# A four-layer graph network on one core: a pair's score vector reaches all partitions through DRAM instead of TensorE transposes

## The chip, the core and the metric

The kernel runs on one core of a Trainium2 chip. The time is that of the device for one launch, in microseconds, and the median of three launches is given. The core has five engines with an instruction queue each: TensorE (PE: matrix products and transposes, which write to PSUM), VectorE (DVE), ScalarE (ACT), GpSimd (POOL) and SyncE (SP), whose queue issues almost all DMA transfers of this kernel. Each of SBUF's and PSUM's 128 partitions holds one row of a tile. [...]

## The reference

`x` is 128 graphs of 128 nodes with 512 features, and `adj` is a 128x128 matrix for each graph. Four layers follow one another, and each ends with a residual sum and a layer norm. Two of them build a score for each pair of nodes out of two vectors, one value per row and one per column:

```python
# layer 0
Xw = X @ Wv + bv
sj = Xw @ aw[:d, 0]
si = Xw @ aw[d:, 0]
e = leaky_relu(sj[:, None, :] + si[:, :, None] + ab[0], negative_slope=0.2)
alpha_matrix = A * exp(e)
transition = alpha_matrix / (sum(alpha_matrix, axis=-1, keepdims=True) + 1e-12)
for k in range(3):
    H = H + Xk @ Wk[k] + bk[k]
    Xk = einsum('bij,bjd->bid', transition, Xk)
# x = layernorm(x + relu(H))

# layer 2
y = x @ w
s = y @ a
A = s[..., :, None] + s[..., None, :]
A = tanh(A / 8.0) * 8.0
A = where(A >= 0, A, 0.1 * A)
A = exp(A) * A_shape
A = A / sum(A, axis=-1, keepdims=True)
A = A * sum(A_shape, axis=-1, keepdims=True)
out = A @ x @ w
```

Layer 1 is a hypergraph convolution and layer 3 is attention with eight heads. The change doesn't touch them. In the kernel, layers 2 and 3 run as one stage.

## The kernel before

The kernel handles graphs in pairs (`U = 2`), so each layer has 64 pairs, and two pairs at a time go through its stages together. It is written as a list of operations with keys, which a planner in the kernel puts into one order for each engine before the program is built. The planner also gives the operations their buffers. A tile of the kind `four` is 128 partitions of 1024 floats, `sq` holds a pair's two 128x128 matrices, `col` holds a few numbers per partition, and `bank` is one buffer of PSUM.

```python
U = 2
BUFS = 12
SQS = 8          # buffers of kind sq
COLS = 32
ROWS = 4         # buffers of kind row (512 floats)
...
WHEN0 = (-3.0, -1.6, -1.0, 0, 0)              # keys of the stages of layer 0
WHENT = (.8, 2.1), (2.0, 3.1)                 # layer 0: scores of the two pairs; their use
WHEN2 = (-2.4, -2.0, -1.45, -1.15, -.7, .3, .5, 2)   # stages of layers 2 and 3
```

A key counts in pairs. The first number of `WHEN2` is for the loads of layer 2, the second for its scores, the third for the first product with the finished matrix.

This brings a pair's score vector to all partitions. A column of 128 values, one in each partition, is read as a 128x128 matrix whose columns are all alike; its transpose has that vector in every row:

```python
def spread_pair(srcs):
    pt = bank()
    with plan.together():
        for b, s in enumerate(srcs):
            pe.transpose(pt[:, b * P:(b + 1) * P], s, ident)
    return pt
```

Layer 0 uses it as follows. `R[r]` is the result of the product with the weights, and two of its columns are the scores `sj` (column `3 * P`) and `si` (column `3 * P + 1`):

```python
twice(left, WT["0"], QW, ...)           # two-level Strassen product, seven parts, .28 apart
yield
for r, i in enumerate(both):
    A = load_adj(i)
    plan.key = base + WHENT[0][r]
    s = col(U)
    ac.activation(s, R[r][:, :, 0, 3 * P + 1], AF.Identity, bias=c0)
    pt = spread_pair([R[r][:, b, 0, 3 * P:3 * P + 1].to_broadcast([P, P]) for b in range(U)])
    e = sq()
    for b in range(U):
        ac.activation(e[:, b], pt[:, b * P:(b + 1) * P], AF.Prelu, bias=s[:, b:b + 1], alpha=0.2)
    ac.activation(e, e, AF.Exp)
    den = col(U)
    ...                                  # times A, row sums, reciprocal, scaling (DVE, POOL)
    loads.append(through_dram(e.rearrange("p b (k w) -> p b k w", w=Q), f"e{i}"))
for r, i in enumerate(both):
    plan.key = base + WHENT[1][r]
    x0 = load_rows(x[i:i + U].rearrange("b p f -> p b f"))
    TT = pair_turned(loads[r])           # back from DRAM, transposed by DVE
    for m in (1, 0):
        for b in range(U):
            ...
            pe.matmul(by, TT[:, b], of, start=False, stop=True, skip_group_check=True)
```

Layer 2 uses it as follows:

```python
s2 = col(U)
for b in range(U):
    dot(s2[:, b:b + 1], x2[:, b], wa_b)              # DVE, sum into one value per row
deg = col(U)
ve.tensor_reduce(deg, A, AX.X, OP.add)
pt = spread_pair([s2[:, b:b + 1].to_broadcast([P, P]) for b in range(U)])
F = sq()
for b in range(U):
    ac.activation(F[:, b], pt[:, b * P:(b + 1) * P], AF.Tanh, bias=s2[:, b:b + 1])
ac.activation(F, F, AF.Prelu, alpha=0.1)
ac.activation(F, F, AF.Exp, scale=8.0)
...                                                  # times A, row sums, scaling (DVE, POOL)
FTs.append(through_dram(F.rearrange("p b (k w) -> p b k w", w=Q), f"F{i}", False))
...
FT = pair_turned(load)                               # the next stage
pe.matmul(pt[:, c * P:(c + 1) * P], x2[:, b, c * P:(c + 1) * P], FT[:, b], start=True, stop=True)
```

`through_dram` writes a matrix to DRAM in blocks and gives a function that loads it back with the blocks rearranged; `pair_turned` then transposes 32x32 blocks on DVE. All instructions are called from one line of the planner, so the profile gives them all the line L369, and they are told apart by their tiles.

Of the kernel before, what the change touches and what calls it, by code (L numbers as in the profile page):

```python
# [13 lines left out]
AF = mybir.ActivationFunctionType  # L14
# [3 lines left out]
P = 128  # L18
# [7 lines left out]
EPS = 1e-5  # L26
U = 2
BUFS = 12
SQS = 8
COLS = 32  # L30
ROWS = 4
KS = 4
OUTS = 4

# [3 lines left out]
WHEN1 = (-3.0, -2.3, -1.6, -1.1, .2, .6)  # L38
STEP1 = .22
WHENH, WHENW, WHENG = (2.4, 3.0), (2.9, 3.6), (3.6, 4.3)  # L40
WHEN2 = (-2.4, -2.0, -1.45, -1.15, -.7, .3, .5, 2)
WHENV, WHENS, WHENP, WHENO = (.9, 1.9), (2.2, 3.2), (3, 4), (3.5, 4.5)
LAG1, LAG2 = 1, 1.5
SOFT = .2
# [333 lines left out]
def kernel(  # L378
# [21 lines left out]
    for kind, (n, _) in spans.items():  # L400
        places[kind] = [first[:, at(kind, k):at(kind, k) + SIZE[kind]] for k in range(n)]
        if kind != "w7":
            for k in range(n):
                later[kind, k] = [(old, i) for old in (("q3", "h") if kind == "q7" else ("w7",))
                                  for i in range(spans[old][0])
                                  if at(old, i) < at(kind, k) + SIZE[kind] and at(kind, k) < at(old, i) + SIZE[old]]
    slots = {"w7": 7, "out": OUTS, "q7": 0, "q3": 0, "h": 0, "w28": 0, "sq": SQS, "col": COLS, "row": ROWS, "bank": 6, "t0": 1, "t1": 1,
             "four": BUFS, "row1": 1, "k": KS}
# [11 lines left out]
    for kind, k, t in (*(("out", k, t) for k, t in enumerate(outs)), ("w28", 0, places["w28"][0]),  # L420
                       ("row1", 0, places["row1"][0])):
        for c in range(SIZE[kind] // SIZE["four"]):
            later["four", len(places["four"])] = [(kind, k)]
            places["four"].append(t[:, c * SIZE["four"]:(c + 1) * SIZE["four"]])
    plan = Plan(slots, later)
    pe, ve, ac, po, sp = (plan.engine(*e) for e in ((PE, nc.tensor), (DVE, nc.vector), (ACT, nc.scalar),
                                                     (POOL, nc.gpsimd), (SP, nc.sync)))

    def tile_of(kind, *shape):
        n = math.prod(shape)  # L430
        flat = View(Tile(kind), np.arange(SIZE[kind]))[:, :n]
        names = [f"a{k}" for k in range(len(shape))]
        return flat if len(shape) == 1 else flat.rearrange(
            f"p ({' '.join(names)}) -> p {' '.join(names)}", **dict(zip(names, shape)))
# [5 lines left out]
    def bank():  # L440
        return tile_of("bank", D)

    def four():

        return tile_of("four", U, D)

    def sq(n=P):
        return tile_of("sq", U, n)

    def col(*n):  # L450
        return tile_of("col", *n)
# [3 lines left out]
    ident = View(Tile("fixed", ident_), np.arange(P))  # L455
# [9 lines left out]
    def row():  # L465
        return tile_of("row", D)
# [205 lines left out]
    def scratch(name, *shape):  # L672
        t = tc.dram_tile(list(shape), FP, name=name)
        return Tile("dram", t)

    def part(tile, how, first, n=1):
        return View(tile, np.arange(first, first + n), (how,))
# [22 lines left out]
    def from_dram(src, kind):  # L700

        nj, _, n = src.shape
        t = kind().rearrange("p u f -> p (u f)").rearrange("p (m j w) -> p m j w", m=4, j=nj)
        for j in range(nj):
            with plan.together():
                for k in range(4):
                    sp.dma_start(t[k * Q:(k + 1) * Q, :, j],
                                 src[j].rearrange("(m r) (k w) -> k r m w", r=Q, k=4)[k],
                                 run=n // 4, parts=Q)
        return t.rearrange("p m j w -> p (m j w)")  # L710
# [64 lines left out]
                for d, v, y in zip(sides(*((0, 1), (1, 1))[j == T3]), sides(1, 0), sides(1, 1)):  # L775
                    po.tensor_tensor(d, v, y, OP.add)

    def spread_pair(srcs):
        pt = bank()
        with plan.together():  # L780
            for b, s in enumerate(srcs):
                pe.transpose(pt[:, b * P:(b + 1) * P], s, ident)
        return pt

    def pair_turned(load):
        t = sq()
# [14 lines left out]
    bias = row().rearrange("p (h n i) -> p h n i", h=2, n=2)  # L801
# [92 lines left out]
    def layer0(i0):  # L894


        both = [i0 + U * r for r in range(2)]
        xbs = [from_dram(x[i:i + U], four) for i in both]
        yield
        xT, loads = [], []  # L900
        for xb in xbs:
            xT.append(four().rearrange("p u (c n) -> p u c n", n=P))
            turned(xT[-1].rearrange("p u c n -> p (u c) n"), xb)
        yield
        left = lefts(xT)
        yield
        base = plan.key
        add = ve.tensor_tensor
        R = [tile_of("out", U, 4, QW) for _ in range(2)]

        def fresh(bs):
            def takes(d):
                def put(d, b):
                    def run(p):
                        ac.copy(d[:, P:], p[:, P:])
                        add(d[:, :P], p[:, :P], b, OP.add)
                    return run
                d11, d12, d21, d22 = d
                return plain_take(*d) | {"p1": put(d11, bs[:, 0]), "v": put(d12, bs[:, 1]),
                                         "p5": put(d22, bs[:, 1]), "c21": put(d21, bs[:, 0])}  # L920
            return takes

        twice(left, WT["0"], QW, lambda r, half: [R[r][:, b, 2 * half + n] for b in range(U) for n in range(2)],
              lambda r, half: [R[r][:, b, 2 * half:2 * half + 2] for b in range(U)],
              [fresh(bias[:, half]) for half in range(2)], .28)
        yield
        loads = []
        for r, i in enumerate(both):
            A = load_adj(i)
            plan.key = base + WHENT[0][r]  # L930
            s = col(U)
            ac.activation(s, R[r][:, :, 0, 3 * P + 1], AF.Identity, bias=c0)
            pt = spread_pair([R[r][:, b, 0, 3 * P:3 * P + 1].to_broadcast([P, P]) for b in range(U)])
            e = sq()
            for b in range(U):
                ac.activation(e[:, b], pt[:, b * P:(b + 1) * P], AF.Prelu, bias=s[:, b:b + 1], alpha=0.2)
            ac.activation(e, e, AF.Exp)
            den = col(U)
            for b in range(U):
                ve.scalar_tensor_tensor(e[:, b], e[:, b], 1.0, A[:, b], op0=OP.mult, op1=OP.mult,  # L940
                                        accum_out=den[:, b:b + 1])
            ac.activation(den, den, AF.Identity, bias=tiny)
            ve.reciprocal(den, den)
            for b in range(U):
                po.tensor_scalar(e[:, b], e[:, b], den[:, b:b + 1], None, op0=OP.mult)
# [4 lines that stand above are left out]
            TT = pair_turned(loads[r])  # L950
            for m in (1, 0):
                for b in range(U):
                    p = tile_of(("t0", "t1")[b], D)
                    by = p.rearrange("p (q i) -> p q i", i=P)
                    to, of = (R[r][:, b, :, k * P:(k + 1) * P] for k in (m, m + 1))
                    ac.copy(by, to)
                    pe.matmul(by, TT[:, b], of, start=False, stop=True, skip_group_check=True)
                    if m:
                        ac.copy(to, by)
                    else:  # L960
                        ve.scalar_tensor_tensor(x0[:, b], p, 0.0, x0[:, b], op0=OP.max, op1=OP.add)
                        layer_norm(x0[:, b])
                plan.key += .2
            sp.dma_start(x1d[i // U], x0)
# [151 lines left out]
    cols = fixed(2, C, name="cols2")  # L1116
# [51 lines left out]
    def layer23(i0):  # L1168
# [10 lines left out]
        for i, x2, A in each(both, x2s, As):  # L1179
            s2 = col(U)  # L1180
            for b in range(U):
                dot(s2[:, b:b + 1], x2[:, b], wa_b)
            deg = col(U)
            ve.tensor_reduce(deg, A, AX.X, OP.add)
            pt = spread_pair([s2[:, b:b + 1].to_broadcast([P, P]) for b in range(U)])
            F = sq()
            for b in range(U):
                ac.activation(F[:, b], pt[:, b * P:(b + 1) * P], AF.Tanh, bias=s2[:, b:b + 1])
            ac.activation(F, F, AF.Prelu, alpha=0.1)
            ac.activation(F, F, AF.Exp, scale=8.0)  # L1190
            r = col(U)
            for b in range(U):
                ve.scalar_tensor_tensor(F[:, b], F[:, b], 1.0, A[:, b], op0=OP.mult, op1=OP.mult,
                                        accum_out=r[:, b:b + 1])
            ve.reciprocal(r, r)
            for b in range(U):
                po.tensor_scalar(F[:, b], F[:, b], r[:, b:b + 1], deg[:, b:b + 1], op0=OP.mult, op1=OP.mult)
            FTs.append(through_dram(F.rearrange("p b (k w) -> p b k w", w=Q), f"F{i}", False))
        yield
        opss = []  # L1200
        for load, x2 in each(FTs, x2s):
            FT = pair_turned(load)
            GT = four().rearrange("p u (c n) -> p u c n", n=P)
            for b in range(U):
                pt = bank()
# [24 lines left out]
        vs = [four() for _ in range(2)]  # L1230
        base = plan.key - WHEN2[6]

# [93 lines left out]
    n = B // U  # L1326
# [21 lines left out]
    for job, start, step in ((prepare2, 2 * n + LAG1 - .3, .1), (prepare_w, 2 * n + LAG1, 0),  # L1348
                             (prepare3, 2 * n + LAG1 + 2, .1)):
        plan.key = start  # L1350
        for k, _ in enumerate(job()):
            plan.key = start + step * (k + 1)
    layer(layer23, 2 * n + LAG1 + LAG2, WHEN2, ramp, size=2)
    ctx.enter_context(tc.manual_schedule())
# [29 lines left out]
```

## Time and profile before

| | us |
|---|---|
| median of three launches | 5482.09 |
| lowest, highest | 5477.86, 5486.19 |
| span of the profiled launch | 5477.4 |
| PE busy in it | 5346.1 |
| DVE busy | 4549.0 |
| POOL busy | 4037.1 |
| ACT busy | 2397.3 |

By the instructions in it, layer 0 takes the span up to about 1400 us, layer 1 up to about 3100 us, and layers 2 and 3 the rest. Between them lie stretches in which weights are prepared. The page gives an engine's busy time as the union of its instructions' times; matrix products overlap in TensorE, so a product's own duration is longer than the time until the next one starts. PEld is the loading of the stationary operand, which overlaps with PE as well. A name such as `bank<-ident,col` is the tile written, then the tiles read, without buffer numbers. The idle time ahead of an instruction is put down to whatever event came last before it began. A DMA's landing is counted from its issue to its completion.

### The profile page before, as it was taken

The numbers are of one execution on the slowest core, as the hardware profiler recorded it, in microseconds if no ns is written. First come the engines' busy times: TensorE is split into PE (matmuls) and PEld (weight loads), VectorE is DVE, ScalarE is ACT, GpSimd is POOL, SyncE is SP. The second block draws the span as 40 slices with busy tenths as digits, with TensorE's granted clock in tenths as the row PEclk, the third lists the DMA queues.
The fourth block names the chain that finished last, engine by engine and source line by source line (L and its number), as shares of the span: only waits on it lengthen the run. The fifth ranks groups of instructions, "written<-read, shape, count | busy, mean of one in ns | idle before, by whom it ended". The sixth has DMA issues, their size and how long they took to land.

```text
span 5477.4 us, 94041 instructions
## 1 busy us (share of the span) xinstructions
PE 5346.1 (98%) x29145; PEld 4258.7 (78%) x29145; DVE 4549.0 (83%) x11553; ACT 2397.3 (44%) x6479; POOL 4037.1 (74%) x4835
## 2 busy tenths in 40 slices
PE   7999999999999999999999999999999999999998
PEld 4555555555788888888888789899999999999987
DVE  6888887878998899998999978777778777877876
ACT  2444343444443434443434345444455445445444
POOL 6666666666777777777777567777777777777776
PEclk8999999999999999999999999999999999999999
DMA  3333333334554544544454545554454555555553
GB/s 92 98 100 98 104 94 107 93 98 126 153 152 144 155 141 151 155 144 151 149 151 148 161 132 164 160 163 153 161 162 155 162 164 152 161 165 156 161 155 119
DMA packets 788381, 768.35 MB, mean 140 GB/s; under 512 B 264859, under 2 KB 592547, under 8 KB 787878
## 3 DMA queue, kind: packets, MB, share of 16 engines
q1 hardware_dynamic: 786374, 759.71, 45.3%
q8 instruction: 231, 3.78, 0.3%
q10 hardware_dynamic: 1504, 2.62, 0.2%
q14 instruction: 272, 2.23, 0.1%
HBM read 435.83 MB, written 326.24 MB: 139 GB/s over the span
## 4 chain that ended last, share of the span: by engine, by line
PE 56%; DVE 7%; DMA 3%; POOL 2%; issue 1%; ACT 1%; SPq 1%; DVEq 0%; POOLq 0%; ACTq 0%
PE bank L369 42%; PE t L369 14%; DVE first L369 2%; DVE col L369 2%; DVE out L369 1%; DVE four L369 1%; POOL out L369 1%; SPq L369 1%; DMA out<-h 1%; DMA h<-first 1%; DMA out<-x3d 1%; POOL first L369 0%; DMA first<-x3d 0%; ACT first L369 0%; DVE junk L369 0%
## 5 line engine op out<-in xcount | busy, mean ns | idle before, releaser
L369 PE MATMUL bank<-first,four 128*128 128x386 f32 (+3 forms) x5176 | 1438.1, 431 | 32.5 <-DVE out L369 14.2
L369 PEld LDWEIGHTS bank<-first,four 128*128 128x128 f32 (+2 forms) x5176 | 846.3, 187 | 588.6 <-DVE out L369 141.5
L369 DVE TENSOR_TENSOR out<-bank,out 128x386 f32<-128x386 f32 (+1 forms) x1884 | 926.6, 509 | 275.5 <-PE bank L369 215.6
L369 POOL TENSOR_TENSOR out<-out 128x256 f32<-128x256 f32 (+3 forms) x482 | 548.6, 1149 | 297.3 <-DVE out L369 214.0
L369 POOL TENSOR_TENSOR col<-col,neghalf 128x1 f32<-128x1 f32 x640 | 378.8, 597 | 375.6 <-DVE col L369 373.9
L369 DVE TENSOR_TENSOR first<-bank,first 128x256 f32<-128x256 f32 x1362 | 542.1, 412 | 129.6 <-PE bank L369 99.0
L369 PE MATMUL bank<-first,out 128*128 128x256 f32 (+2 forms) x2560 | 623.4, 381 | 25.7 <-DVE first L369 10.1
L369 PEld LDWEIGHTS bank<-first,out 128*128 128x128 f32 (+1 forms) x2560 | 469.4, 190 | 127.3 <-DVE first L369 30.6
L369 PE MATMUL bank<-four,out 128*128 128x256 f32 (+2 forms) x2118 | 538.1, 376 | 2.9 <-DVE col L369 1.4
L369 DVE TENSOR_TENSOR four<-bank,four 128x256 f32<-128x256 f32 x818 | 337.7, 417 | 142.9 <-PE bank L369 128.3
L369 PE MATMUL bank<-out,first 128*128 128x128 f32 (+2 forms) x2840 | 427.8, 290 | 2.2 <-DVE out L369 1.2
L369 ACT COPY out<-bank 128x258 f32<-128x258 f32 (+2 forms) x555 | 236.6, 431 | 419.7 <-PE bank L369 378.6
L369 PEld LDWEIGHTS bank<-four,out 128*128 128x128 f32 (+2 forms) x2118 | 369.7, 189 | 59.1 <-issue 8.4
L369 PEld LDWEIGHTS bank<-out,first 128*128 128x128 f32 (+1 forms) x2840 | 374.4, 188 | 26.0 <-DVE four L369 2.8
L369 ACT ACTIVATE col<-col,col 128x1 f32<-128x1 f32 x640 | 183.2, 292 | 456.2 <-POOL col L369 390.1
L369 POOL TENSOR_TENSOR four<-four,four 128x256 f32<-128x256 f32 (+2 forms) x395 | 329.0, 837 | 13.0 <-DVE four L369 3.2
L369 ACT COPY t<-out 128x512 f32<-128x512 f32 x256 | 150.2, 591 | 421.9 <-DVE four L369 217.6
L369 POOL TENSOR_TENSOR first<-first 128x512 f32<-128x512 f32 (+3 forms) x196 | 232.2, 1197 | 110.3 <-DVE first L369 73.9
L369 POOL TENSOR_TENSOR out<-out,out 128x256 f32<-128x256 f32 (+2 forms) x286 | 288.2, 1011 | 9.3 <-DVE four L369 4.4
L369 POOL TENSOR_TENSOR four<-four 128x256 f32<-128x256 f32 (+2 forms) x331 | 244.3, 754 | 67.6 <-DVE four L369 38.3
L369 POOL TENSOR_SCALAR sq<-sq,col 128x128 f32<-128x128 f32 x256 | 160.5, 636 | 153.4 <-DVE col L369 149.0
L369 DVE BATCH_NORM_STATS2 col<-first 128x6 f32<-128x512 f32 x370 | 245.5, 681 | 27.2 <-ACT first L369 25.4
(406 smaller groups left out, 12715.2 us busy)
## 6 DMA issues: line engine op xcount, KB each, us to landing
h<-first SPq DMA_DIRECT2D x496, 128.0 KB, 2.4
out<-x1d SPq DMA_DIRECT2D x88, 512.0 KB, 4.3
out<-h SPq DMA_DIRECT2D x87, 512.0 KB, 4.6
four<-in_x_dram SPq DMA_DIRECT2D x512, 64.0 KB, 2.0
four<-in_x_dram SPq DMA_DIRECT2D x62, 512.0 KB, 3.5
x1d<-four SPq DMA_DIRECT2D x62, 512.0 KB, 2.7
first<-S SPq DMA_DIRECT2D x61, 512.0 KB, 4.4
out<-S SPq DMA_DIRECT2D x50, 512.0 KB, 4.4
```

The lines of the kernel that those rows point to most:

```text
L369: call(*map(real, args), **{n: real(a) for n, a in kw.items()})
```

## The change

The score vector of a pair is written from its column to a small array in DRAM, one row of 128 values per graph. Then one load reads both rows, 256 values, into every one of the 128 partitions. The tile `sq` that holds them takes the place of the PSUM bank as the source of ScalarE's first operation. This takes the transposes of layers 0 and 2 away from TensorE. The other transposes of the kernel stay, those of weights, of vectors that are spread once, and of the last attention. Two more `sq` buffers are given, two `row` buffers are taken away, and the first two stages of layer 2 are keyed earlier.

```diff
-SQS = 8
+SQS = 10
 COLS = 32
-ROWS = 4
+ROWS = 2
...
-WHEN2 = (-2.4, -2.0, -1.45, -1.15, -.7, .3, .5, 2)
+WHEN2 = (-2.5, -2.2, -1.45, -1.15, -.7, .3, .5, 2)
...
-    def spread_pair(srcs):
-        pt = bank()
-        with plan.together():
-            for b, s in enumerate(srcs):
-                pe.transpose(pt[:, b * P:(b + 1) * P], s, ident)
-        return pt
+    def spread_pair(cols, name):
+
+        d = scratch(name, U, P)
+        sp.dma_start(part(d, lambda t: t.rearrange("b p -> p b"), 0), cols, run=1)
+        t = sq()
+        sp.dma_start(t.rearrange("p b n -> p (b n)"),
+                     part(d, lambda t: t.rearrange("(x b) p -> x (b p)", x=1).to_broadcast([P, U * P]), 0), run=U * P)
+        return t
...
-            pt = spread_pair([R[r][:, b, 0, 3 * P:3 * P + 1].to_broadcast([P, P]) for b in range(U)])
+            pt = spread_pair(R[r][:, :, 0, 3 * P], f"s{i}")
             e = sq()
             for b in range(U):
-                ac.activation(e[:, b], pt[:, b * P:(b + 1) * P], AF.Prelu, bias=s[:, b:b + 1], alpha=0.2)
+                ac.activation(e[:, b], pt[:, b], AF.Prelu, bias=s[:, b:b + 1], alpha=0.2)
...
-            pt = spread_pair([s2[:, b:b + 1].to_broadcast([P, P]) for b in range(U)])
+            pt = spread_pair(s2, f"s2{i}")
             F = sq()
             for b in range(U):
-                ac.activation(F[:, b], pt[:, b * P:(b + 1) * P], AF.Tanh, bias=s2[:, b:b + 1])
+                ac.activation(F[:, b], pt[:, b], AF.Tanh, bias=s2[:, b:b + 1])
```

## The prediction

> **What bounds the kernel now.** I read the page's busy shares first, then the busy time by stage, then every instruction that has `ident` as an operand (the transposes), then stretches of the timeline around single pairs, and last the DMA issues and the waits of the DMA queue. The page:
>
> ```profile
> PE 5346.1 (98%) x29145; PEld 4258.7 (78%) x29145; DVE 4549.0 (83%) x11553; ACT 2397.3 (44%) x6479; POOL 4037.1 (74%) x4835
> ```
>
> The share alone hides stages, so here is the busy time in one stretch each of layer 0, of layer 1 and of layers 2 and 3 (stretch and its length, then PE, PEld, DVE, ACT and POOL busy with their counts, granted clock, DMA share, GB/s):
>
> ```profile
> 500.00:1000.00 500.00, 499.23 (x1489) 270.52 (x1488) 408.08 (x1041) 204.24 (x475) 338.07 (x401) 1.00 0.34 102
> 1600.00:2600.00 1000.00, 981.04 (x4689) 825.43 (x4688) 902.30 (x2231) 405.09 (x760) 775.81 (x909) 1.00 0.50 150
> 3500.00:5000.00 1500.00, 1495.58 (x11102) 1367.17 (x11101) 1196.56 (x3175) 739.98 (x2520) 1161.76 (x1432) 1.00 0.51 160
> ```
>
> In both stages that the change touches TensorE is busy over 99.7% of the time, at full clock. Work taken off it there should leave the span, unless it is replaced by a wait. The other engines have room: DVE is at 82% and 80%, ACT at 41% and 49%, the DMA engines at 34% and 51%.
>
> The transposes, with min/median/max duration, and those who waited for them:
>
> ```profile
> L369 PE MATMUL bank<-ident,out x168: 271/273/473, 55.9 to 5448.1; 128*128 128x128 f32 x168
> ...
> L369 PE MATMUL bank<-ident,col x66: 272/273/323, 3088.4 to 5327.3; 128*128 128x128 f32 x66
> ...
> L369 PE MATMUL t<-ident,col x62: 272/273/273, 3230.9 to 5187.9; 128*128 128x128 f32 x62
> ...
> who waited for it (us, times):
>   ACT sq L369: 137.2, 77
> ```
>
> The 66 + 62 = 128 with `col` are layer 2's (64 pairs of two). Layer 0's are most of the 168 with `out`; the rest of those belong to weights and to the last attention. The 137 us of ACT's waiting cost nothing by themselves: ACT is far from the bound.
>
> The 273 ns of a record is a latency, not what it costs TensorE. That is the distance between starts. A pair in layer 0, and one in layer 2 (start us, us, what):
>
> ```profile
> 738.89 1.14 PE L369 MATMUL bank<-first,four 128*128 128x386 f32 x3
> 739.86 0.38 PE L369 MATMUL bank<-ident,out 128*128 128x128 f32 x2
> 740.08 1.21 PE L369 MATMUL bank<-first,four 128*128 128x386 f32 x3
> ```
>
> ```profile
> 4012.69 0.61 PE L369 MATMUL bank<-out,first 128*128 128x128 f32 x4
> 4013.14 0.38 PE L369 MATMUL bank<-ident,col 128*128 128x128 f32 x2
> 4013.45 0.82 PE L369 MATMUL bank<-out,four 64*128 64x128 f32 x9
> ```
>
> In layer 0 a pair takes 740.08 - 739.86 = 0.22 us of TensorE. In layer 2 it looks like 0.31 us, but what follows are 64-row products of the attention. In eight places of this trace a 64-row group follows an ordinary 128x128 product with no transpose between, and its start is 0.20 us later in place of the usual 0.11. So 0.09 of the 0.31 is the switch to 64 rows, which stays; the pair itself is 0.22 us here too.
>
> **What the Trainium skill says.** (1) "TensorE: Matmul & The Clock Gate", Part 4: PE-mode transpose, gives about 275 ns for a transpose in a kernel's context, mostly access latency. The trace agrees (273 ns), and shows besides that the next instruction starts after 0.11 us, so I don't multiply by 275. (2) "DMA: Bandwidth & Descriptors", Rules for kernel authors: a DMA that reads what an earlier one wrote must wait for that one's completion. So the added path is two whole DMAs in series. (3) The same page, Anatomy of one DMA, puts a fixed cost of about 2 us on each, most of it completion at the target memory. The landings below agree for small transfers (1.5 to 2.1 us), while those of many pieces are longer. (4) The same rules say that a strided last dimension becomes one descriptor per element. The score write goes to two DRAM rows from 128 partitions, so I take it as 256 pieces of 4 bytes.
>
> **The change part by part.** *Removed:* two transposes in each of 64 pairs in layer 0 and 64 in layer 2; the instruction order of the changed kernel confirms that exactly 256 go, and nothing else of TensorE. 128 pairs x 0.22 us = 28.2 us (with 0.218, the median over layer 0's pairs, 27.9). All of it lies on the engine that is busy 99.7%, so I count it whole: -28 us. A PSUM buffer for about 1 us per pair goes as well.
>
> *Added:* per pair one score write, a wait, and one broadcasting load of 128 rows of 1 KB. Their nearest relatives in the trace (KB each, median us to landing):
>
> ```profile
> bv_c<-in_L_gnn_bv_dram SPq DMA_DIRECT2D x1, 2.0 KB, 6.1
> ...
> e<-sq SPq DMA_DIRECT2D x512, 16.0 KB, 1.5
> sq<-e SPq DMA_DIRECT2D x64, 128.0 KB, 2.1
> ...
> F<-sq SPq DMA_DIRECT2D x128, 64.0 KB, 5.3
> sq<-F SPq DMA_DIRECT2D x64, 128.0 KB, 2.0
> ```
>
> A write `e` is 128 pieces, so I take 2 us for 256 pieces of 4 bytes; the load has the shape of `sq<-e`, 2.1 us. With the second issue about 4.5 us from a finished score to scores on all partitions, where a transpose slot and ACT's start cost about 0.5 us: each pair's chain grows by 4 us. In layer 2, where `F` takes 5.3 us (two writes of 512 pieces), I allow 6 us.
>
> *Does this fit?* In layer 0 the first pair's score column is final after the second of the seven products of its two-level multiplication, .28 of a step after the stage's start, while its transposes are keyed .8; a step is about 19 us (pairs repeat at 39 us for two). So some 10 us of slack lie before the removed transposes. The second pair's column is final at 1.68 and keyed at 2.1, 8 us. In layer 2 the scores of the pair above were made here:
>
> ```profile
> 4005.36 0.69 DVE L369 SCALAR_TENSOR_TENSOR junk<-out,row 128x512 f32<-128x512 f32 x1
> ...
> 4005.98 0.08 DVE L369 DVE_READ_ACCUMULATOR junk<-out,row 128x1 f32 x1
> 4005.98 0.41 DVE L369 TENSOR_REDUCE col<-sq 128x2 f32<-128x256 f32 x1
> ```
>
> and the transposes ran at 4013.14: 7 us of waiting for a place in TensorE's order, into which two DMAs just fit. The change also moves layer 2's loads and scores up (from -2.0 to -2.2 of a step of about 35 us, 7 us more). So I book no steady wait, and +2 us for single late ones at the layers' edges.
>
> *Lesser terms:* the issues take 128 x 2 x 0.43 = 110 us of SyncE's queue, spread over 3400 us. Packets: 128 x (256 + 128) = 49,000 on 788,000, 6%; at the page's mean (45.8% of 16 engines' span over all packets, 51 ns) at most 156 us of all engines' time, 3% of the span. The extra two score buffers replace two unused row buffers. The ten instead of eight let a pair hold one buffer longer.
>
> Sum: 5482.1 - 28 + 2 = 5456 us, 0.5% less.
>
> **The rivals.** *A: a DMA wait takes the transposes' place.* SyncE issues in order, so waiting for a score write holds every load behind it:
>
> ```profile
> SPq L369 <- DMA F<-sq: 263.8, 67, 6.1
> ```
>
> It stands 264 us for `F` already without starving TensorE, which speaks against. If half of the pairs lost 0.3 us on TensorE, 20 us come back: 5475. If all lost 0.5 us, the time would be some 5520; the 7 to 10 us of slack make that unlikely. *B: longer landings of large loads by the extra packets*, mainly in layer 2 at a share of 0.51. TensorE hardly waits for DMA there now; I would expect 5 to 10 us lost at most, 5465. *C: more gained than counted.* A PSUM buffer and a fixed place in TensorE's order are set free, and the whole order is built anew. TensorE's 131 us of idling lie mostly in layer 1, the transitions and the tail; 10 to 15 of these might go, 5440.
>
> **Range and chances.** A new order of some 28,000 instructions moves single waits by ten or so us either way, which is wider than the spread of the three times (5478 to 5486). Eight in ten: 5438 (C in full) to 5478 (A for half of the pairs). For 2% either way the time would have to pass 5372, nearly four times what is removed, or 5592, which needs a new wait of 1 us at every pair. Chances: faster by over 2% 0.01, within 2% 0.97, slower by over 2% 0.02.
>
> **What would show it.** Right: 256 records fewer with `ident`; TensorE's busy time about 28 us less, 15 in layer 0 and 14 in layer 2; its share in both stages still over 99%; ACT's wait for TensorE at `sq` gone, and in its place one for a DMA. Wrong: a TensorE wait at `t<-out,sq` or `bank<-sq,out` of more than a few us in total; score writes that land after 5 us or more in layer 0; SyncE's waits for score writes followed by TensorE's idling for late loads.

## The result, and the profile after

| | us | ratio to before (95% interval) |
|---|---|---|
| before | 5481.2 (in the runs beside the changed kernel) | |
| changed | 6124.6 (6115.7 to 6137.2) | 1.1175 (1.1152 to 1.1197) |
| predicted | 5456 (5438 to 5478) | |

The change makes the kernel 643 us slower. The transposes are gone: 256 matrix instructions are missing. Yet TensorE is busy for longer, and for a smaller share of the span. The page of the changed kernel:

```profile
PE 5549.4 (91%) x28889; PEld 4365.1 (71%) x28889; DVE 4594.0 (75%) x11553; ACT 2395.5 (39%) x6479; POOL 4083.9 (67%) x4835
```

The busy time by stage shows where. These are stretches in layer 0, in layer 1, and in layers 2 and 3 (columns as before the change):

```profile
500.00:1000.00 500.00, 441.01 (x1193) 233.28 (x1192) 338.79 (x858) 170.94 (x391) 280.83 (x332) 0.94 0.34 90
2000.00:3000.00 1000.00, 981.24 (x4690) 826.93 (x4690) 898.39 (x2253) 410.41 (x770) 779.99 (x910) 1.00 0.50 148
4000.00:5500.00 1500.00, 1353.67 (x9472) 1213.14 (x9471) 1062.63 (x2733) 630.97 (x2164) 1023.23 (x1231) 0.95 0.55 140
```

Layer 1, which has no score vector, is as it was. In layer 0 TensorE does 1193 products in 500 us where it did 1489, a fifth fewer. It idles 59 us of the 500, where it idled 0.8, and its granted clock falls to 0.94. The products last longer: in that stretch the mean of a 128x386 product is 514 ns in place of 490, and of a 128x512 product 633 in place of 594. That is why busy time rises while work falls. Note the last two columns of layer 0: the DMA engines are as busy as before (0.34), but move 90 GB/s in place of 102. By the share alone nothing has changed; per byte they are busy for 13% longer.

The landings show more. DMA issues of the changed kernel (KB each, median us from issue to landing):

```profile
sq<-in_adj_dram SPq DMA_DIRECT2D x128, 128.0 KB, 6.1
sq<-s SPq DMA_DIRECT2D x128, 128.0 KB, 5.2
...
s<-out SPq DMA_DIRECT2D x64, 1.0 KB, 8.1
...
s<-col SPq DMA_DIRECT2D x64, 1.0 KB, 8.5
```

Of the kernel before, the load of `adj` and a store that is needed below:

```profile
x1d<-four SPq DMA_DIRECT2D x62, 512.0 KB, 2.7
...
sq<-in_adj_dram SPq DMA_DIRECT2D x128, 128.0 KB, 3.2
```

A score write of 1 KB takes 8.1 us in layer 0 and 8.5 in layer 2, longer than any load of 512 KB on the same list that runs in the same layers. The 128 KB load of `adj`, which only happens to be issued near it, went from 3.2 to 6.1 us; in `settings` below, which has the numbers of the change and no score writes, it takes 3.8. What the DMA queue and ScalarE waited for (us in total, times, longest us), in the queue's own list of waits and in that of all engines:

```profile
SPq L369 <- DMA s<-out: 400.2, 63, 8.9
SPq L369 <- DMA s<-col: 356.9, 59, 9.6
```

```profile
ACT sq L369 <- DMA sq<-s: 569.5, 110, 11.5
```

One pair of layer 0 shows how this reaches TensorE. The timeline of SyncE's queue (start us, us, what):

```profile
587.73 0.38 SPq L369 DMA_DIRECT2D x1d<-four  x1
590.85 0.36 SPq L369 DMA_DIRECT2D s<-out  x1
591.25 0.47 SPq L369 DMA_DIRECT2D sq<-in_adj_dram  x1
599.23 0.33 SPq L369 DMA_DIRECT2D sq<-s  x1
```

GpSimd, ScalarE, VectorE and TensorE in the same stretch, in that order (in brackets the idle time ahead and what ended it):

```profile
598.84 1.26 POOL L369 TENSOR_TENSOR four<-four 128x512 f32<-128x512 f32 x1 [9.54 <-DMA sq<-in_adj_dram]
```

```profile
601.32 0.29 ACT L369 ACTIVATE col<-col,col 128x1 f32<-128x1 f32 x1 [7.27 <-POOL col L369]
```

```profile
603.02 0.29 DVE L369 TENSOR_TENSOR out<-bank,row 128x128 f32<-128x128 f32 x1 [8.79 <-ACT out L369]
```

```profile
594.10 1.56 PE L369 MATMUL bank<-first,four 128*128 128x386 f32 x4 [0.40 <-ACT out L369]
603.37 2.94 PE L369 MATMUL bank<-first,four 128*128 128x386 f32 x4 [7.71 <-DVE out L369]
```

And the landings of the two transfers issued between 590.8 and 591.8:

```profile
sq<-in_adj_dram SPq DMA_DIRECT2D x1, 128.0 KB, 8.1
s<-out SPq DMA_DIRECT2D x1, 1.0 KB, 8.3
```

The score write was issued at 590.85 and the load that needs it could go at 599.23. GpSimd stood too, for 9.54 us, and not for the scores. The profile names the load of `adj`: of the completion counters at which the instruction looks, the one stepped by this load moved last. But that load landed 8.1 us after its issue, at 599.3, when GpSimd was already at work. The other transfer for which this instruction waits is the store `x1d<-four`. It was issued at 587.73, 3.1 us ahead of the score write, and by the trace its completion counter was full at 598.68, 11 us later. ScalarE waited for GpSimd, VectorE for ScalarE, TensorE for VectorE: 7.71 us of idling. So there are two suspects, the waiting for the scores and the harm that the write does to other transfers, even to one issued before it.

### The profile page after: what moved, and what is told of

The parts are those of the page before. It is cut to its first block, busy times and chain, and to the rows that moved or that the text cites. A ratio compares the mean times of both kernels' runs of the same rounds, so it can differ in the third digit from the quotient of the medians.

```text
span 6126.0 us, 94176 instructions
## 1 busy us (share of the span) xinstructions
PE 5549.4 (91%) x28889; PEld 4365.1 (71%) x28889; DVE 4594.0 (75%) x11553; ACT 2395.5 (39%) x6479; POOL 4083.9 (67%) x4835
## 5 line engine op out<-in xcount | busy, mean ns | idle before, releaser
L369 PE MATMUL bank<-first,four 128*128 128x386 f32 (+2 forms) x5136 | 1587.6, 459 | 167.2 <-DVE out L369 114.7
L369 PEld LDWEIGHTS bank<-first,four 128*128 128x128 f32 (+1 forms) x5136 | 954.5, 196 | 766.8 <-DVE out L369 179.2
L369 PE MATMUL bank<-four,out 128*128 128x256 f32 (+2 forms) x1926 | 459.3, 368 | 5.5 <-ACT first L369 2.6
L369 POOL TENSOR_TENSOR four<-four,four 128x256 f32<-128x256 f32 (+2 forms) x484 | 415.0, 864 | 29.6 <-DVE four L369 14.8
L369 PE MATMUL bank<-out,first 128*128 128x128 f32 (+2 forms) x2172 | 343.5, 289 | 7.0 <-DVE four L369 2.2
L369 PE MATMUL bank<-four,four 128*128 128x256 f32 (+2 forms) x1488 | 311.9, 351 | 33.9 <-ACT four L369 11.7
L369 ACT ACTIVATE sq<-sq,col 128x128 f32<-128x128 f32 x256 | 89.6, 394 | 609.3 <-DMA sq<-s 569.5
L369 PEld LDWEIGHTS bank<-out,first 128*128 128x128 f32 (+1 forms) x2172 | 298.0, 194 | 27.1 <-DVE four L369 4.5
L369 PE MATMUL t<-out,sq 128*128 128x512 f32 x512 | 271.0, 635 | 49.1 <-ACT t L369 28.4
L369 ACT COPY out<-t 128x512 f32<-128x512 f32 (+1 forms) x287 | 148.3, 517 | 390.1 <-PE t L369 389.7
```

Of the source, the lines that this page charges most:

```text
L369: call(*map(real, args), **{n: real(a) for n, a in kw.items()})
```

## The experiments

Each ratio is to the kernel before, run on the same chip. At the outset there were four theories. A: the score write completes late, and the waiting for it costs. B: the broadcasting load is late by itself. C: the new numbers of buffers and the new keys spoil the order. D: the added packets slow all transfers. The first runs led to a fifth, E: 4-byte pieces that are neighbours in DRAM hold each other up, and other transfers with them.

**A write that nobody reads, in four layouts.** The kernel before keeps its transposes and gets a score write besides:

```diff
+    width, n = (1, 16, 128, 1)[kind], (U, U, U, 1)[kind]       # kind goes round by pairs
+    d = scratch(name, n, P, width)
+    sp.dma_start(part(d, lambda t: t.rearrange("b p w -> p b w")[:, :, 0], 0), cols[:, :n], run=1)
```

> The kernel before, transposes and all, plus a score write per pair that nobody reads, in four layouts in turn: 256 pieces of 4 bytes side by side (one, as in the change), the same 64 bytes apart (line), 512 bytes apart (wide), and only one graph's 128 pieces side by side (half). Theory A (the write itself is slow to complete, and it is the waiting for it that costs): the time stays within 0.5% of before, and one lands after about 8 us. Two forms of A: if pieces in one stretch of DRAM hold each other up, line and wide land after 2 to 3 us and half after 5; if the number of pieces decides, line and wide land after 8 too and half after 5. Theory D (the added packets slow all transfers): the time rises by 3% or more though nobody waits.

Measured: 5709.5 us, 1.0411 (1.0396 to 1.0427). That is 226 us lost though nothing waits for the scores. The landings can be read from the completion counters in the trace: the transfers take eight counters in turn, and one transfer steps its counter 16 times, so the last step before the counter's next use is the landing. (For the score writes for which the view above has a landing, both agree to about 0.2 us.) The medians in layer 0 are 9.9 us side by side, 1.6 at 64 bytes, 1.7 at 512 bytes, and 8.0 for one graph's 128 pieces side by side. Half of the pieces is not half of the time. What a layout costs is seen from runs with one layout each, below.

**The load waits for no write.**

```diff
-                     part(d, ...to_broadcast([P, U * P]), 0), run=U * P)
+                     x[i0, 0:1, :U * P].to_broadcast([P, U * P]), run=U * P)
```

> The changed kernel, but the broadcasting load reads 256 values of one row of the input x in place of the score vector, so it waits for no write; the write is still made and nobody reads it. The scores are therefore other numbers. Theory A (the late write): 5450 to 5490 us, as predicted for the change itself. Theory B (the broadcasting load by itself, in which 128 partitions read one stretch of 1 KB, is late and holds ScalarE): the load lands after 5 us still, and the time stays above 5750. Theory C (the new buffer counts and keys spoil the order) or D (traffic): above 6000.

Measured: 6214.2 us, 1.1331 (1.1308 to 1.1354). ScalarE still waits 329 us for this load, which needs no score. So the loss is not the load's wait for its write.

**The planner is told.** It counts 5.5 us more until a score write is complete and 2.5 us more for the load.

```diff
-        sp.dma_start(part(d, ..., 0), cols, run=1)
+        sp.dma_start(part(d, ..., 0), cols, run=1, late=5500)
...
-                     part(d, ...to_broadcast([P, U * P]), 0), run=U * P)
+                     part(d, ...to_broadcast([P, U * P]), 0), run=U * P, late=2500)
```

> The changed kernel with the same transfers, but the planner is told that the score write completes 5.5 us and the broadcasting load 2.5 us later than it assumes for a transfer of that size. Theory A in the form that the order was built for a wrong latency: most of the loss comes back, 5460 to 5600 us, with landings as before (8 and 5 us). If the longer chain itself can't be hidden in any order (too few buffers, too little slack): above 5750. Theory C or D: no change, about 6100.

Measured: 6172.5 us, 1.1251 (1.1234 to 1.1267), with landings of 9.3 and 9.7 us for the writes and 6.2 for the load. ScalarE's wait for the scores fell from 570 to 265 us, and SyncE's for the writes from 757 to 378 us. The time didn't fall. An order built for the long latency does not help: half of the waiting for the scores went and no time with it. That no order at all could hide so long a chain is not excluded by this run; the next one and `gap16` keep the chain and lose the cost.

**The write in eight pieces of 128 bytes.** VectorE turns the column in blocks of 32, so each of four partitions holds 32 scores of each graph side by side.

```diff
-        sp.dma_start(part(d, lambda t: t.rearrange("b p -> p b"), 0), cols, run=1)
+        blk = tile_of("blk", U, Q)
+        ve.transpose(blk, cols[:, :, None].to_broadcast([P, U, Q]))
+        sp.dma_start(part(d, lambda t: t.rearrange("b (k r) -> k b r", r=Q), 0), blk[::Q], run=Q, parts=P // Q)
```

> The changed kernel, but VectorE first turns the score column in blocks of 32, so that the write is eight pieces of 128 bytes from four partitions in place of 256 of 4 bytes. Theory A (late write of many small pieces): it lands after about 2 us and the time is 5450 to 5500. Theory B (the load): the load lands after 5 us still and the time stays above 5750. Theory C: about 6100. Theory D: some two thirds of the loss comes back with two thirds of the packets gone, about 5700.

Measured: 5499.0 us, 1.0029 (1.0019 to 1.0039). 97% of the loss is gone with the two transfers still in series. The waits of the DMA queue for the score write fall from 757 us to this:

```profile
SPq L369 <- DMA s<-blk: 94.8, 98, 3.7
```

**The same 256 pieces, side by side or 64 bytes apart.** Two kernels with the same instructions in the same order, both the kernel before plus an unread write per pair. They differ in a number of the scratch array's shape:

```diff
+        d = scratch(name, U, P, 1)       # unread_one: pieces side by side
+        d = scratch(name, U, P, 16)      # unread_line: 64 bytes apart
+        sp.dma_start(part(d, lambda t: t.rearrange("b p w -> p b w")[:, :, 0], 0), cols, run=1)
```

> The kernel before, transposes and all, plus for each of the 128 pairs one score write that nobody reads, 256 pieces of 4 bytes side by side as in the change. In the run with four layouts 64 of the 128 writes had their pieces side by side, and it took 226 us more. New theory E (4-byte pieces that lie side by side in DRAM hold each other up while they complete, and the transfers behind them on the DMA engines stand): all 128 writes cost about twice that, 5900 to 5950 us, with no one waiting for the scores. If it was the waiting for the scores after all: 5490 to 5520.

> The same kernel and the same order of instructions, with the same 256 pieces of 4 bytes per write; only the places in DRAM lie 64 bytes apart. Theory E: close to before, 5483 to 5510 us. Theory D (the number of small packets is what costs): 5900 to 5950, like its twin.

Measured: side by side 6077.8 us, 1.1082 (1.1059 to 1.1105); 64 bytes apart 5498.0 us, 1.0024 (1.0015 to 1.0033). This pair settles what costs. The number of pieces, their size, the bytes moved and the order are the same, and 580 us hang on whether the pieces are neighbours in DRAM. Side by side, in layer 0 and in layers 2 and 3:

```profile
500.00:1000.00 500.00, 449.93 (x1243) 239.78 (x1244) 344.81 (x867) 169.78 (x392) 282.85 (x333) 0.92 0.46 86
...
3700.00:5200.00 1500.00, 1370.35 (x9741) 1223.49 (x9740) 1061.51 (x2787) 654.01 (x2218) 1023.12 (x1256) 0.97 0.52 140
```

and in its twin in layer 0:

```profile
500.00:1000.00 500.00, 499.20 (x1488) 270.34 (x1487) 407.34 (x1041) 204.07 (x475) 337.83 (x402) 1.00 0.36 101
```

For TensorE this is nearly the picture of the changed kernel, with all transposes in place and no one waiting for a score. Here the DMA engines do show it, with a share of 0.46 for 86 GB/s in place of 0.36 for 101. The engines' waits in it that end with a transfer:

```profile
POOL out L369 <- DMA out<-x3d: 161.3, 32, 9.2
DVE sq L369 <- DMA sq<-e: 123.4, 35, 7.6
POOL four L369 <- DMA x1d<-four: 107.5, 25, 7.7
POOL four L369 <- DMA four<-x3d: 90.5, 18, 7.6
```

and in the twin:

```profile
POOL out L369 <- DMA out<-x3d: 11.0, 12, 2.0
...
POOL four L369 <- DMA four<-x3d: 9.4, 10, 1.9
DVE sq L369 <- DMA sq<-e: 9.3, 11, 2.3
```

All of these are other transfers, loads and stores. Single names can be wrong, as in the pair above, but the sums are some ten times those of the twin. The longest waits, 7.6 to 9.2 us, are about as long as a score write's landing. By the counters the store `x1d<-four` lands after 9.6 us (median) in place of 2.8 in the twin. The writes of the twin land so:

```profile
linea<-out SPq DMA_DIRECT2D x64, 1.0 KB, 1.6
...
lineb<-col SPq DMA_DIRECT2D x64, 1.0 KB, 1.5
```

By the counters, those of layer 0 that lie side by side take 9.9 us. And though nobody reads them, SyncE's queue waits for them:

```profile
SPq L369 <- DMA oneb<-col: 125.7, 33, 6.2
SPq L369 <- DMA onea<-out: 118.5, 44, 8.7
```

With eight counters in turn, a transfer isn't issued before the one eight places ahead of it has landed. In the twin no such wait is listed. So an unread write does harm in two ways, by the later landing of other transfers and by holding up the queue for 244 us. How the 594 us divide between the two isn't shown.

**How far apart is far enough?** 32 bytes in layer 0, 16 bytes in layer 2:

```diff
+        d = scratch(name, U, P, 8 if at == "a" else 4)
```

> The kernel before plus the unread score writes again, now with the 4-byte pieces 32 bytes apart in layer 0 and 16 bytes apart in layer 2. Side by side they cost 594 us, 64 bytes apart 14 us. Theory E (neighbours in one stretch of DRAM hold each other up): if the stretch is 64 bytes, two or four pieces meet in one and the loss is a part of the full one, 5500 to 5750, with landings between 2 and 8 us; if distance as such must reach 64 bytes, the loss is whole, about 6000; if any gap is enough, below 5510.

Measured: 5495.3 us, 1.0028 (1.0017 to 1.0040), as little as with 64 bytes. The landings:

```profile
gapa<-out SPq DMA_DIRECT2D x64, 1.0 KB, 1.8
gapb<-col SPq DMA_DIRECT2D x64, 1.0 KB, 2.2
```

So in layer 0 the landing is 1.6 us at 64 bytes and 1.8 at 32; in layer 2 it is 1.5 at 64 bytes and 2.2 at 16. Side by side it is 8.1 and 8.5 in the changed kernel, and up to 9.9 in the other runs (medians). It grows a little as the distance shrinks, and leaps between 16 and 4 bytes.

**The spacing undone in the changed kernel itself.** The pieces lie 16 bytes apart, and the load brings the gaps along:

```diff
-        sp.dma_start(part(d, lambda t: t.rearrange("b p -> p b"), 0), cols, run=1)
-        t = sq()
+        d = ring[i // U % 16]             # 16 arrays of U x P x 4, set to zero once
+        sp.dma_start(part(d, lambda t: t.rearrange("b p w -> p b w")[:, :, 0], 0), cols, run=1)
+        t = four().rearrange("p u f -> p (u f)")
...
+        return t.rearrange("p (b n w) -> p b n w", n=P, w=4)[:, :, :, 0]
```

> The changed kernel with the same 256 pieces of 4 bytes, now 16 bytes apart, into arrays that are set to zero once; the broadcasting load brings the gaps along (4 KB to each partition in place of 1 KB), and ScalarE reads every fourth value. Theory E: the write lands after about 2.2 us, and nearly all of the loss is gone although the loads move 67 MB more: 5470 to 5620 us. If it is the two transfers in series or the small pieces as such, whatever their distance: above 5900.

Measured: 5500.8 us, 1.0034 (1.0021 to 1.0047). The same 4-byte pieces, the same two transfers in series, the same numbers of buffers and keys, and loads four times as large: all but 18 of the 643 us are gone. The landings:

```profile
s<-out SPq DMA_DIRECT2D x64, 1.0 KB, 2.7
s<-col SPq DMA_DIRECT2D x64, 1.0 KB, 3.5
```

**The numbers alone, and layer 0 alone.** `settings` is the kernel before with `SQS`, `ROWS` and `WHEN2` of the change; `layer0_only` is the changed kernel with the transposes back in layer 2.

```diff
-SQS = 8
+SQS = 10
-ROWS = 4
+ROWS = 2
-WHEN2 = (-2.4, -2.0, ...
+WHEN2 = (-2.5, -2.2, ...
```

```diff
-            pt = spread_pair(s2, f"s2{i}")
+            pt = spread_by_pe([s2[:, b:b + 1].to_broadcast([P, P]) for b in range(U)])
```

> The kernel before with its transposes, and of the change only the numbers: ten score buffers, two row buffers, the earlier keys of layer 2. Theory E: these are harmless, 5460 to 5510 us. Theory C (the numbers spoil the order): above 5550.

> The changed kernel with layer 2 back on TensorE transposes, so half of the score writes. Theory E: cost by the number of writes, near the middle between before and after, 5700 to 5850 us. If the loss came from layer 2 alone, where the DMA engines are busier: below 5500.

Measured: the numbers alone 5492.4 us, 1.0015 (1.0008 to 1.0023), so they cost 8 us beside transposes. Layer 0 alone 5847.2 us, 1.0657 (1.0641 to 1.0673): 363 us for half of the writes, so both layers pay.

**What becomes of the saving once the write is repaired.** Pieces of 128 bytes in one layer alone, then with other keys:

```diff
 # rows32_l0: transposes in layer 2; rows32_l2: transposes in layer 0
 # rows32_keys, both layers:
-WHEN2 = (-2.5, -2.2, ...
+WHEN2 = (-2.4, -2.0, ...
 # lead (both layers) and lead_l2 (layer 2 alone):
-WHEN2 = (-2.5, -2.2, ...
+WHEN2 = (-2.7, -2.4, ...
```

> The write in eight pieces of 128 bytes in layer 0 alone; layer 2 keeps its transposes. With both layers it took 5499 us. If the 28 us of removed transposes are real but the newly built order loses as much in other places: 5480 to 5500, with TensorE 14 us less busy. If the load path itself costs layer 0 time: above 5500.

> The write in eight pieces of 128 bytes in layer 2 alone; layer 0 keeps its transposes. If the pieces of 128 bytes make the path harmless and layer 2 keeps its gain: 5470 to 5490 us. If layer 2, with the DMA engines at half load, is where the new path costs: above 5500.

> The write in eight pieces of 128 bytes in both layers, with the old keys of layer 2 (-2.4 and -2.0) and the new numbers of buffers. The new numbers alone cost 8 us beside transposes. If the keys are to blame for what the repaired path loses: 5460 to 5485 us. If the extra lead is needed for the path through DRAM: above 5500.

> The write in eight pieces of 128 bytes in both layers, with loads and scores of layer 2 keyed earlier still (-2.7 and -2.4). The old keys gave 5636, those of the change 5499. If the chain through DRAM still lacks lead: 5465 to 5490 us, mostly from layers 2 and 3. If the lead is enough and the rest is the rebuilt order's: 5490 to 5520, or worse where tiles are held longer.

> The same earlier keys with the DRAM path in layer 2 alone, written in 128-byte pieces (5482 us with the keys of the change). If lead is lacking: 5460 to 5475 us, below the kernel before. If not: 5478 to 5500.

| 128-byte pieces in | keys | us | ratio (95%) |
|---|---|---|---|
| both layers | -2.4, -2.0 | 5636.5 | 1.0285 (1.0268 to 1.0302) |
| both layers | -2.5, -2.2 | 5499.0 | 1.0029 (1.0019 to 1.0039) |
| both layers | -2.7, -2.4 | 5475.8 | 0.9987 (0.9980 to 0.9994) |
| layer 0 | -2.5, -2.2 | 5492.9 | 1.0019 (1.0012 to 1.0027) |
| layer 2 | -2.5, -2.2 | 5481.8 | 1.0002 (0.9993 to 1.0011) |
| layer 2 | -2.7, -2.4 | 5484.3 | 0.9999 (0.9990 to 1.0008) |

With the old keys TensorE waits for the finished matrix of layer 2, 40 us in nine waits; in `lead` this wait is 1.7 us. TensorE's waits with the old keys:

```profile
PE bank L369 <- DVE sq L369: 40.1, 9, 12.1
```

With the most lead, the repaired path is the only version whose interval lies below the kernel before, by 7 us. In layer 2 alone the same lead gains nothing (5484.3 against 5481.8), so how much of the 23 us between the second and third rows is lead, and how much the newly built order, isn't shown. Its page and three stretches, of layer 0, of layer 1 and of layers 2 and 3:

```profile
PE 5323.9 (97%) x28889; PEld 4239.5 (77%) x28889; DVE 4583.5 (84%) x11681; ACT 2381.6 (44%) x6479; POOL 4076.6 (74%) x4835
```

```profile
500.00:1000.00 500.00, 493.88 (x1441) 269.02 (x1440) 407.37 (x1068) 205.85 (x474) 340.07 (x403) 1.00 0.38 108
1700.00:2700.00 1000.00, 987.06 (x4722) 831.04 (x4721) 900.39 (x2249) 409.02 (x764) 785.73 (x916) 1.00 0.50 149
3700.00:5200.00 1500.00, 1484.39 (x10948) 1346.78 (x10946) 1215.61 (x3191) 717.48 (x2514) 1178.29 (x1420) 1.00 0.53 162
```

TensorE's busy time is 5346.1 - 5323.9 = 22 us less than before, close to the 28 of the prediction. But its idle time grew from 5477.4 - 5346.1 = 131.3 us to 5473.7 (the span of this profile) - 5323.9 = 149.8 us, so 18.5 of the 22 us are given back. The stretches show where: in layer 0 it idles 6.1 us of 500 where it idled 0.8, and in layers 2 and 3 15.6 of 1500 where it idled 4.4. The removed work is real, and most of it comes back as short waits in the two stages that the new path runs through.

## Why the prediction was wrong

**What bounds the kernel: right.** Where TensorE was busy 99.7%, it was what counted. It is also how a write that nobody reads could cost 594 us: with no idle time to hide in, stops of other engines can reach TensorE, as in the pair shown, where 9.54 us of GpSimd became 7.71 of TensorE.

**What is removed: right.** 256 instructions went. 0.22 us a pair, 28 us in all, is near the size seen in TensorE's busy time once the new path does no harm (22 us in `lead`).

**What is added: here the prediction failed.** The step was "A write `e` is 128 pieces, so I take 2 us for 256 pieces of 4 bytes". It measured 8.1 and 8.5 us, past the 5 us that the prediction had named as a sign of being wrong. The relative was chosen by the number of pieces, and what decides is their neighbourhood: the pieces of `e` are 128 bytes long. The same 256 pieces 64 bytes apart landed in 1.6 and 1.5 us, so 2 us would have been a fair figure for the spaced layouts. The load, sized as `sq<-e` at 2.1 us, took 5.2. `F`, at 5.3 us before, was no warning of this: with the transposes in place and only the numbers changed (`settings`) the same write lands after 2.5 us.

**The lesser terms: the larger failure.** I sized the packets by the mean time of a packet, as 3% of the DMA engines' span in total, and called that harmless. For the number of packets this was right: spaced out, the same packets cost 14 us. (The four queues of the page add up to 45.9%, not 45.8; nothing hangs on it.) But a write of side-by-side pieces makes other transfers near it land late and holds SyncE's queue, and neither is in that sum. `unread_one` gives the size: 594 us over 128 writes, 4.6 us for each. With 8 for the new numbers and 28 less for the transposes, 574 of the changed kernel's 643 us are accounted for, if these simply add. The waits for the scores may be the rest, but that isn't shown: `no_wait`, which is without them, took longer still.

**The slack: right, and beside the point.** The chain's length was called hidden by 7 to 10 us of slack. With 128-byte pieces it is, if layer 2 gets its lead; the old keys cost 161 us more than the earliest ones (5636.5 against 5475.8), so the lead of the change was necessary and not enough. In the changed kernel itself latency was not the cost: telling the planner of it did not help (6172.5 us).

**The rivals.** A (a DMA wait in the place of the transposes) was seen, 757 us in SyncE's queue and 570 in ScalarE's, but it isn't the loss: taking the load's wait away left 6214 us. B (longer landings of large loads by the extra packets) had the effect right and its cause wrong: other transfers do land later, but not by the number of packets, and stores as well as loads, in layer 0 as in layer 2. It was put down for 5 to 10 us because TensorE hardly waited for DMA before. That was the wrong evidence. The waits arose at GpSimd, ScalarE and VectorE, through which the products' results pass. C did not come.

**What stays open.** Why neighbours hold each other up isn't shown. The Trainium skill ("DMA: Bandwidth & Descriptors", Specifications) says that transfers of under 512 bytes are read-modify-writes; no run here shows it. That alone would not be it, since 4-byte pieces 16 bytes apart land in 2.2 us. That such writes follow one another where several of them meet in one stretch of DRAM is a guess, and that one graph's 128 pieces take 8.0 us where both graphs' 256 take 9.9 speaks against a plain sum over all pieces. A distance of 8 bytes, and pieces of 8 or 16 bytes side by side, weren't tried. Nor is it shown where between issue and landing the other transfers stand.

## What to carry to other kernels

A column of single values from 128 partitions should not be written to adjacent words of DRAM: first turn it so that a piece is a row of 32 (here one VectorE instruction), or leave a gap. A transfer is not free because nobody reads it: compare the landings of the transfers around it, since the busy share of the DMA engines alone can stay as it was (0.34 here). And test a suspected transfer by adding it, unread, to the kernel before: it separates in one run what the transfer does to others, and to the queue, from what waiting for its data costs.

## What the runs showed of the hardware

- 256 pieces of 4 bytes from 128 partitions, written to DRAM, land after 1.5 to 1.6 us when 64 bytes apart, 1.8 at 32, 2.2 at 16 (2.7 and 3.5 in `gap16`, beside larger loads), and 8.1 to 9.9 when side by side.
- With such side-by-side writes, other transfers land late (`x1d<-four` after 9.6 us, by the counters, in place of 2.8 in the twin kernel; longest waits of 7.6 to 9.2 us for transfers for which no wait exceeds 2.3 us there). The DMA engines' busy share in layer 0 was 0.46 in place of 0.36 in this pair, and 0.34 as before in the changed kernel, in both cases for fewer bytes.
- A broadcasting load in which all 128 partitions read one stretch of 1 KB landed after 5.2 us in the changed kernel; the 4 KB version beside spaced writes landed after 4.8 to 5.5 us, so the load by itself was not what cost.
- Short stops of TensorE, 12% idle in layer 0, came with a granted clock of 0.94 in place of 1.00 and products that lasted 5 to 7% longer (490 to 514 and 594 to 633 ns).
